# A two-layer graph network with a mixture of experts: thirds, selection matrices, products and routing moved to other steps

## The chip, the cores and the metric

The kernel runs on one core of a Trainium2 chip. The core has five engines that work side by side, each through its own instructions in order: TensorE (PE in the profile; its weight loads are PEld), VectorE (DVE), ScalarE (ACT), GpSimd (POOL) and SyncE (SP), which issues transfers. They wait for each other by semaphores. Times are microseconds (us) on the device. The number to be predicted is the median time of the changed kernel; the kernel before has a median of 3390.55 us over 3 runs (3386.48 to 3399.7).

## The reference, cut to what matters

There are 6250 nodes with 512 features, 100,000 edges sorted by their destination, and 8 experts.

```python
def _sage_layer(h, src, dst, W_self, W_neigh, b, n_nodes):
    agg = segment_sum(h[src], dst, n_nodes)
    deg = segment_sum(ones_like(dst), dst, n_nodes)
    h_neigh = agg / maximum(deg, 1.0)[:, None]
    return relu(h @ W_self + h_neigh @ W_neigh + b)

x = x + sage_layer2(sage_layer1(layernorm(x)))
xf = layernorm(x)                       # again, then a mixture of experts
logits = xf @ Wg
topv, topi = top_k(logits, 2)
gate_w = softmax(topv)
h = relu(xf @ W1[e] + b1[e])            # per expert e
y = h @ W2[e] + b2[e]
y = (y - mean) / sqrt(var + EPS) * gamma[e] + beta[e]
x = x + sum over the two chosen experts of gate_w * y
```

## The kernel before, in words

**Stages.** A first pass (up to about 117 us) normalizes the nodes and makes tables of the edges. Then `sums` runs twice: in stage 1 over the rows of the normalized nodes (layer 1, from about 120 to 1115 us), in stage 2 over the projected rows of layer 1 (layer 2, from about 1138 to 2340 us). A tail computes the remaining expert tiles and combines.

**What `sums` does.** The 782 tiles of 128 edges are taken in 197 steps of four tiles (`while` loop from L300). In step i GpSimd issues the gathers of step i + 2 (`gather`, L220): each fetches 128 rows of 512 numbers. The buffers of gathered rows form a ring, so a gather waits until `add` of three steps before has read its buffer. `build` (L230) makes, on VectorE, the zero-one matrices ("hot") of step i + 2. `add` (L248) multiplies them with the gathered rows on TensorE: each tile gives up to 32 destination rows, and the four tiles of a step lie under each other in one bank of PSUM, pa. Three steps make a round, 66 rounds in all. At the end of a round `close` copies pa into a bf16 strip on ScalarE (L258). `rest` makes the second and third strip out of what rounding left (L272 on VectorE, L273 on ScalarE, L274 on VectorE), so that three bf16 thirds hold the f32 sum. When a round is the last that can touch a block b of 128 nodes, `prepare` makes the block's selection matrices on VectorE (L280, one for each of its two to four rounds), and `take_out` multiplies the strips by them on TensorE (L290), two steps after the round has closed. In stage 1 `take_out` writes to a tile ps and also takes the degrees (pn); in stage 2 it writes to a tile named ph.

**What sets the order.** The order on TensorE, VectorE, ScalarE and GpSimd is the order of the code (`manual_schedule`). Work that follows later is put into a table with a step and a place: `at(i, place, what)`. In every step the loop issues the gathers, lets `each(i)` register new work, builds, adds, runs the "mid" list of that step, closes a round, and runs the "post" list. Within one list the work stands in the order in which it was registered, so what was registered longest ago comes first.

**Layer 1** (`layer1`) registers the products with the layer's weights after a take-out (u0 to u5, L557 and the transposes at L194).

**Layer 2** (`route`) follows each take-out of stage 2. VectorE finishes the block's rows (L1003, L1004), their mean and variance (L182, L184), ScalarE the root (L186), and VectorE the normalized rows xn (L187, L1011). Then `turn` transposes xn on TensorE (L194, copied by ScalarE at L196), `logits` multiplies by Wg (L958, copied at L960), `experts` transposes the logits and chooses two experts on VectorE and ScalarE (L964, L966, L654 to L669), `rank` counts the nodes of each expert (L976, L977 on TensorE; L979 to L987 on VectorE), and `send` scatters the rows to the experts' lists by GpSimd (L991). The tiles that logits, experts and rank write are all named small, with one bank.

**Expert tiles in stage 2** (`each`, `Up`, `Down`). As soon as enough lists are known (at step 76), an expert tile of 128 rows begins at every second step. `Up.fetch` reads the rows xg by SP (L812), `turn_x` transposes them (L194, L196), `times` is the up product (L824, eight TensorE passes, into a tile ph; copied by ScalarE to h at L827), `turn_h` transposes h (L832) and adds the bias with a relu on VectorE (L835). Every second tile ("soon") goes on at once: `Down` builds its on VectorE (L847), `times` is the down product (L858, eight passes, and L852 for the row b2, into py), `spread` takes mean and variance on VectorE (L864, L866) with a root on ScalarE (L868), `scale` normalizes (L871, L873, then L876 on ScalarE), `affine` makes the rows of gamma and beta on TensorE (L852, into two tiles ph) and `finish` multiplies and adds them on VectorE (L882, L883) and stores y by SP. The other tiles keep hT in memory for the tail. PSUM tiles named ph come in two buffers, those named pt in two.

**Share of layer 2.** Until step 48, `share_of` (L923) multiplies the stored layer 1 rows in three steps of four.

The registrations that the change touches are these, before:

```python
at(i + 1, "mid", lambda pa=pa[0]: rest(st, k, pa))
at(i + 1, "mid", lambda b=b: prepare(b))
at(i + 2, "mid", lambda b=b: take_out(i + 2, b))
todo = [(2, "mid", turn), (3, "mid", logits), (4, "mid", experts), (5, "post", rank), ...
todo = [(0, "post", u.fetch), (3, "mid", u.turn_x), (4, "mid", u.times), (5, "mid", u.turn_h)]
todo += [(7, "mid", begin), (8, "mid", spread), (9, "mid", scale), (10, "post", affine and finish)]
```

Of the kernel before, what the change touches and what calls it, by code (L numbers as in the profile page):

```python
# [29 lines left out]
F32 = mybir.dt.float32  # L30
# [9 lines left out]
P = 128  # L40
# [27 lines left out]
def gnn_moe(ctx, tc, x, src, dst, Ws1, Wn1, gb1, Ws2, Wn2, gb2, Wg, W1, b1, W2, b2, gamma, beta, out):  # L68
    nc = tc.nc
    N, D = x.shape  # L70
# [4 lines left out]
    HC = H // P  # L75
# [124 lines left out]
    def sums(z, pool, pap, room, pn, finish, ring, nring, each=None):  # L200

        nslot = (NG - 1) * TS + min(TS, NT_E - (NG - 1) * NQ * TS)
        ahead = nring // NQ - 1
        tiles = [[t for t in range(i // TS * NQ * TS + i % TS, min(NT_E, (i // TS + 1) * NQ * TS), TS)]
                 for i in range(nslot)]
        gathered, hots, few, strips, counts, sels, due = {}, {}, {}, {}, {}, {}, {}  # L210
        pa = [None]

        def at(i, place, what):
            due.setdefault((i, place), []).append(what)

        def gather(i):
            if i < nslot:
                for t in tiles[i]:
                    gathered[t] = ring()
                    nc.gpsimd.indirect_dma_start(  # L220
                        out=gathered[t], out_offset=None, in_=z[:, :],
                        in_offset=bass.IndirectOffsetOnAxis(ap=srcT[:, t : t + 1], axis=0))

        def build(i):
            if i >= nslot:
                return
            g, j = divmod(i, TS)
            m = len(tiles[i])
            hots[i] = pool.tile([P, NQ, SW], F32, name="hot", bufs=3 if pn is None else 4)
            nc.vector.tensor_tensor(  # L230
                hots[i][:, :m],
                rel.rearrange("p (c j) -> p j c", j=TS)[:, j, g * NQ : g * NQ + m]
                .rearrange("p (t o) -> p t o", o=1).to_broadcast([P, m, SW]),
                iota_row[:, :SW].rearrange("p (o m) -> p o m", o=1).to_broadcast([P, m, SW]), OP.is_equal)
            if pn is not None and j:

                end = j == TS - 1 or i == nslot - 1
                few[g] = pool.tile([P, NQ, SW], BF16 if end else F32, name=f"few{int(end)}", bufs=1)
                before = hots[i - 1] if j == 1 else few[g, 1]
                nc.vector.tensor_add(few[g][:, :m], before[:, :m], hots[i][:, :m])  # L240
                few[g, j] = few[g]

        def add(i):
            g, j = divmod(i, TS)
            if pa[0] is None:
                pa[0] = pap.tile([P, D], F32, name="pa", bufs=2)
            for q, t in enumerate(tiles[i]):
                nc.tensor.matmul(pa[0][q * SW : (q + 1) * SW], hots[i][:, q], gathered.pop(t), start=(j == 0),  # L248
                                 stop=(j == TS - 1 or t == NT_E - 1), tile_position=(0, q * SW))

        def close(i):

            g = i // TS
            k = len(tiles[i]) * SW

            st = [pool.tile([P, D], BF16, name=f"st_{h}", bufs=most) for h in range(3)]
            strips[g] = st, k
            nc.scalar.copy(st[0][:k], pa[0][:k])  # L258
            at(i + 1, "mid", lambda pa=pa[0]: rest(st, k, pa))
            pa[0] = None  # L260
            if pn is not None:
                nc.tensor.matmul(pn[:k, 0], few[g].rearrange("p q m -> p (q m)")[:, :k], halves,
                                 start=True, stop=True)
                counts[g] = pool.tile([P, NDEG], BF16, name="counts", bufs=most + 1)
                nc.vector.tensor_copy(counts[g][:k], pn[:k, 0])
            for b in range(NB):
                if reach[b][1] == g:
                    at(i + 1, "mid", lambda b=b: prepare(b))
                    at(i + 2, "mid", lambda b=b: take_out(i + 2, b))

        def rest(st, k, pa):
            nc.vector.tensor_sub(pa[:k], pa[:k], st[0][:k])  # L272
            nc.scalar.copy(st[1][:k], pa[:k])  # L273
            nc.vector.tensor_sub(st[2][:k], pa[:k], st[1][:k])  # L274

        def prepare(b):
            for g in range(reach[b][0], reach[b][1] + 1):
                k = strips[g][1]
                sels[b, g] = pool.tile([P, P], BF16, name="sel", bufs=most)
                nc.vector.tensor_scalar(sels[b, g][:k], iota_row[:k], float(b * P), node[:k, g : g + 1],  # L280
                                        op0=OP.add, op1=OP.is_equal)

        def take_out(i, b):
            a, z = reach[b]
            ps = room()
            for g in range(a, z + 1):
                st, k = strips[g]
                sel = sels.pop((b, g))
                for h in range(3):
                    nc.tensor.matmul(ps, sel[:k], st[h][:k], start=(g == a and h == 0), stop=(g == z and h == 2))  # L290
                if pn is not None:
                    nc.tensor.matmul(pn[:, 1], sel[:k], counts[g][:k], start=(g == a), stop=(g == z))
            for behind, place, what in finish(b, ps) if pn is None else finish(b, ps, pn[:, 1]):
                at(i + behind, place, what)

        for i in range(ahead):
            gather(i)
        build(0)
        build(1)
        i = 0  # L300
        while i < nslot or any(k[0] >= i for k in due):
            gather(i + ahead)
            if each is not None:
                for behind, place, what in each(i):
                    at(i + behind, place, what)
            build(i + 2)
            if i < nslot:
                add(i)
            for what in due.pop((i, "mid"), ()):
                what()  # L310
            if i < nslot:
                if i % TS == TS - 1 or i == nslot - 1:
                    close(i)
            for what in due.pop((i, "post"), ()):
                what()
            i += 1
# [111 lines left out]
    with tc.tile_pool(name="l0", bufs=3, side="right") as pool, \  # L428
# [4 lines left out]
        for lo, hi in ((NS, NB), (0, NS)):  # L433
            full = hi if rows[hi - 1] == P else hi - 1
            at = lo
# [405 lines left out]
    class Down:  # L841
# [10 lines left out]
            nc.tensor.matmul(ps, self.its, thirds[name], start=to is None, stop=True)  # L852
            return ps

        def times(self):
            self.py = self.psp.tile([P, D], F32, name="py", bufs=1 + (self.rows["beta"] == "pb"))
            for c in range(HC):
                nc.tensor.matmul(self.py, self.hT[:, c], w2[:, bass.ds(self.e * KD + c * D, D)],  # L858
                                 start=(c == 0), stop=False)
            self.row("b2", self.py)  # L860

        def spread(self):
            st = self.pool.tile([P, 6], F32, name="st")
# [23 lines left out]
    rest = [i for i in range(NT) if i not in soon]  # L887
# [7 lines left out]
    def fetch_hidden(k):  # L895
        nc.sync.dma_start(part(NW + k % NE), hd[rest[k]])

    with tc.tile_pool(name="s2", bufs=2, side="right") as pool, \
# [32 lines left out]
        def ring():  # L931
            nring[0] += 1
            return part(NW + (nring[0] - 1) % 12)
# [10 lines left out]
        def route(b, pa):  # L944
# [61 lines left out]
            for e in range(NE):  # L1006
                if b == (1 + 3 * e if e < NE // 2 else NB // 4 - 3 + e):
# [2 lines left out]
            t["xn"] = part(NW + (13, 14, 16)[b % 3])  # L1010
            nc.vector.tensor_scalar(t["xn"][:n], acc[:n], mv[:n, 0:1], rs[:n], op0=OP.subtract, op1=OP.mult)  # L1011
            fetch_own(b + 1)
            todo = [(2, "mid", turn), (3, "mid", logits), (4, "mid", experts), (5, "post", rank),
                    (7, "mid", lambda: send(0)), (7, "post", lambda: send(1))]
            if b + 1 in TAKE:
                todo.append((7, "post", take))
# [2 lines left out]
        def each(i):  # L1019


            at_slot[0] = i
            if i == last_slot + 1:
                for k in range(EARLY):
                    fetch_hidden(k)
            q = i - 1 - i // 4
            if i % 4 and q < NS:
                return [(0, "post", lambda: share_of(q))]
            j = up_next[0]
            if i % 2 or j >= upto_n[-1]:  # L1030
                return []
            c = max(c for c in range(len(n0)) if n0[c] <= j)
            if ready.get(c, 1 << 30) > i:
                return []
            up_next[0] += 1
            u = Up(j, pool, psp, keep=j not in soon)
            todo = [(0, "post", u.fetch), (3, "mid", u.turn_x), (4, "mid", u.times), (5, "mid", u.turn_h)]
            if j in soon:
                d = {}

                def begin():
                    d[0] = Down(j, u.hT, u.e, pool, psp, pool.tile([P, D], F32, name="y", bufs=1))
                    d[0].rows = {"gamma": "ph", "beta": "ph"}
                    d[0].times()

                todo += [(7, "mid", begin), (8, "mid", lambda: d[0].spread()), (9, "mid", lambda: d[0].scale()),
                         (10, "post", lambda: (d[0].affine(), d[0].finish()))]
            return todo

        for q in range(3):  # L1050
# [319 lines left out]
```

## Time and profile before

| What | Value |
|---|---|
| median of 3 runs | 3390.55 us (3386.48 to 3399.7) |
| the profiled execution's own time | 2960.86 us |
| its span, first to last instruction | 2958.9 us |
| mean granted TensorE clock | 0.971 |
| TensorE busy | 2647.7 us, 89% of the span |
| GpSimd busy | 1840.5 us, 62% |
| VectorE busy | 1344.7 us, 45% |
| ScalarE busy | 682.4 us, 23% |
| bytes moved | 699.16 MB, mean 236 GB/s |

The profile is of one execution, whose own time is 430 us below the median of the runs shown. In its rows, a line number such as L248 is a line of the kernel, out<-in names the tiles written and read, x is a number of instructions. "Idle before" is the time that an engine stood still just before instructions of that row, with what it waited for behind the arrow; "issue" means that no cause shows. In a list of waits, the numbers are microseconds in total, how often, and the longest. A timeline row has its start, its length and the idle time before it in brackets. A TensorE row's end is modelled, so a row may reach a little into the next. The granted clock is a share of full speed.

### The profile page before, as it was taken

To read this page: it belongs to the slowest core of one execution; us is meant where nothing else is said; L and a number is where in the kernel's file an instruction comes from. 1 tells how busy PE (TensorE), PEld (TensorE's weight loads), DVE (VectorE), ACT (ScalarE), POOL (GpSimd) and SP (SyncE) were. 2 spreads that over 40 slices of the span, in tenths; PEclk is the share of its full clock that TensorE was granted. 3 is DMA by queue.
4 is the path that set the end of the run, shared out by engine and by line. 5 is a ranking of instruction groups with operands and counts; after the bars stand their busy time and mean duration, and the time that the engine had idled before them with its cause. 6 is when DMAs were issued, how large, how long until landed. Compare 5 with 4: busy or idle time off the path is not lost. (4 is left out here: it accounts for less than half of the span.)

```text
span 2958.9 us, 34414 instructions
## 1 busy us (share of the span) xinstructions
PE 2647.7 (89%) x10010; PEld 1035.4 (35%) x10010; DVE 1344.7 (45%) x4274; ACT 682.4 (23%) x1259; POOL 1840.5 (62%) x2116
## 2 busy tenths in 40 slices
PE   6889999999999998999878999899898889999994
PEld 3323333333333333333212333333333333344441
DVE  6523233323323331454335556555655536544774
ACT  2311111111112120121112333333333312222221
POOL 5377777777777763777777777677677118200553
PEclk8999999999999998999989999999999999999997
DMA  6778888888887765999888888888788424212996
GB/s 226 248 238 250 250 250 248 271 245 254 244 252 235 238 205 182 328 327 316 274 280 272 279 271 274 254 271 273 248 273 269 148 84 146 92 57 75 297 299 206
DMA packets 269820, 699.16 MB, mean 236 GB/s; under 512 B 43036, under 2 KB 43150, under 8 KB 269596
## 3 DMA queue, kind: packets, MB, share of 16 engines
q0 software_dynamic: 144000, 464.43, 50.9%
q1 hardware_dynamic: 121964, 225.61, 22.1%
q10 hardware_dynamic: 3664, 6.85, 0.7%
q8 instruction: 85, 1.39, 0.2%
q14 instruction: 107, 0.88, 0.1%
HBM read 557.23 MB, written 140.28 MB: 236 GB/s over the span
## 5 line engine op out<-in xcount | busy, mean ns | idle before, releaser
L220 POOL DMA_INDIRECT big<-z,srcT x782 | 749.6, 959 | 334.5 <-issue 150.1
L220 POOL DMA_INDIRECT rows_t<-xn_d,srcT x782 | 741.1, 948 | 285.2 <-issue 126.7
L248 PE MATMUL pa<-big,hot 128*32 128x512 f32 x1564 | 335.2, 622 | 58.0 <-DMA big<-z,srcT 53.3
L557 PE MATMUL pm<-wn,tT 128*128 128x512 f32 x752 | 347.7, 605 | 0.7 <-ACT tT L196 0.7
L248 PE MATMUL pa<-rows_t,hot 128*32 128x512 f32 x1564 | 275.3, 608 | 24.6 <-DMA rows_t<-xn_d,srcT 23.8
L824 PE MATMUL ph<-big,xg 128*128 x544 | 258.5, 619 | 42.3 <-ACT xg L196 42.0
L1093 POOL DMA_INDIRECT big<-ys,yrow x98 | 107.8, 1100 | 291.2 <-DMA ys<-y 193.1
L858 PE MATMUL py<-w,hT 128*128 x568 | 263.6, 607 | 5.8 <-DVE hT L1146 5.6
L557 PEld LDWEIGHTS pm<-wn,tT 128*128 128x128 f32 x752 | 135.2, 189 | 214.2 <-issue 168.9
L274 DVE TENSOR_TENSOR st<-pa,st 128x512 bf16<-128x512 f32 x132 | 91.2, 691 | 214.3 <-ACT st L273 209.6
L273 ACT CAST st<-pa 128x512 bf16<-128x512 f32 x132 | 77.2, 585 | 416.6 <-DVE pa L272 416.6
L824 PEld LDWEIGHTS ph<-big,xg 128*128 128x128 f32 x544 | 100.5, 195 | 197.3 <-issue 130.4
L858 PEld LDWEIGHTS py<-w,hT 128*128 128x128 f32 x568 | 102.7, 191 | 144.2 <-issue 111.8
L290 PE MATMUL ps<-st,sel 128*128 128x512 bf16 (+1 forms) x459 | 110.2, 379 | 45.8 <-DVE sel L280 45.8
L991 POOL DMA_INDIRECT xs<-big,slot x98 | 98.6, 1006 | 77.2 <-DVE slot L987 47.9
L557 PE MATMUL pm<-ws,big 128*128 128x512 f32 x320 | 146.4, 602 | 0.0
L923 PE MATMUL ph<-w 128*128 128x512 f32 x288 | 135.8, 615 | 5.0 <-DMA w<-in_L_gnn_W_self 5.0
L1134 PE MATMUL ph<-big,xg 128*128 x296 | 136.9, 605 | 0.0
L248 PEld LDWEIGHTS pa<-big,hot 128*32 128x32 f32 x1564 | 51.2, 109 | 234.1 <-DMA big<-z,srcT 165.5
L858 PE MATMUL py<-w,big 128*128 x272 | 127.3, 611 | 4.8 <-DVE y L883 3.8
L290 PEld LDWEIGHTS <-sel 128*128 128x128 bf16 (+1 forms) x918 | 75.8, 98 | 157.6 <-DVE sel L280 63.3
L230 DVE TENSOR_TENSOR hot<-rel,iota_row 128x128 f32<-128x128 bf16 (+1 forms) x394 | 109.7, 283 | 31.2 <-PE pa L248 24.3
(265 smaller groups left out, 3335.0 us busy)
## 6 DMA issues: line engine op xcount, KB each, us to landing
xg<-xs SPq DMA_DIRECT2D x105, 256.0 KB, 4.1
ys<-y SPq DMA_DIRECT2D x105, 256.0 KB, 3.0
rows_t<-xn_d,srcT POOLq DMA_INDIRECT x782
big<-z,srcT POOLq DMA_INDIRECT x782
z<-big SPq DMA_DIRECT2D x48, 256.0 KB, 3.8
xa<-in_x SPq DMA_DIRECT2D x48, 256.0 KB, 5.7
big<-s SPq DMA_DIRECT2D x48, 256.0 KB, 5.4
accs<-xa SPq DMA_DIRECT2D x48, 256.0 KB, 3.9
```

The costliest lines, as they stand in the source:

```text
L220: nc.gpsimd.indirect_dma_start(out=gathered[t], out_offset=None, in_=z[:, :], in_offset=bass.IndirectOffsetOnAxis(ap=srcT[:, t : t + 1], a ...
L230: nc.vector.tensor_tensor(hots[i][:, :m], rel.rearrange("p (c j) -> p j c", j=TS)[:, j, g * NQ : g * NQ + m] .rearrange("p (t o) -> p t o" ...
L248: nc.tensor.matmul(pa[0][q * SW : (q + 1) * SW], hots[i][:, q], gathered.pop(t), start=(j == 0), stop=(j == TS - 1 or t == NT_E - 1), tile ...
L274: nc.vector.tensor_sub(st[2][:k], pa[:k], st[1][:k])
L290: nc.tensor.matmul(ps, sel[:k], st[h][:k], start=(g == a and h == 0), stop=(g == z and h == 2))
L557: nc.tensor.matmul(ph, tT[:, c], w[:, c], start=(start and c == 0), stop=(stop and c == C - 1))
L824: nc.tensor.matmul(ph, self.xT[:, c], w1[:, bass.ds(self.e * KD + c * D, D)], start=(c == 0), stop=(c == C - 1))
L858: nc.tensor.matmul(self.py, self.hT[:, c], w2[:, bass.ds(self.e * KD + c * D, D)], start=(c == 0), stop=False)
L923: nc.tensor.matmul(ps, hT[:, c], ws2[:, c], start=(c == 0), stop=(c == C - 1))
L991: inst = nc.gpsimd.indirect_dma_start(out=xs[:, :], out_offset=bass.IndirectOffsetOnAxis(ap=slot[:n, b, k : k + 1], axis=0), in_=t["xn"][: ...
L1093: nc.gpsimd.indirect_dma_start(out=yk[:n], out_offset=None, in_=ys[: ready[0] * P, :], in_offset=bass.IndirectOffsetOnAxis(ap=yrow[:n, b, ...
L1134: nc.tensor.matmul(ph, u.xT[:, c], w1[:, bass.ds(u.e * KD + c * D, D)], start=(c == 0), stop=(c == C - 1))
```

## The change

The loop gets a third list, "pre", which is run after `each(i)` and ahead of `build(i + 2)` and `add(i)`. These things move:

- `rest` (the second and third strips) goes from the "mid" list of the next step to its "pre" list.
- `prepare` (the selection matrices) goes from the "mid" list of the next step to the "post" list of the step in which the round closes.
- `turn`, `logits` and `experts` of a block go from steps 2, 3 and 4, "mid", to steps 1, 2 and 3, "post". `rank` and `send` stay.
- `Up.fetch` goes from step 0 to step 1, the up product from 4 to 5, `turn_h` from 5 to 6; `turn_x` stays at 3.
- `Down` begins at 7, "post", with the first four passes of its product; the other four and the row b2 follow at 8, "mid". `spread` goes to 8, "post", `scale` to 9, "post", `affine` and `finish` from 10, "post", to 11, "mid".

```diff
-            at(i + 1, "mid", lambda pa=pa[0]: rest(st, k, pa))
+            at(i + 1, "pre", lambda pa=pa[0]: rest(st, k, pa))
...
-                    at(i + 1, "mid", lambda b=b: prepare(b))
+                    at(i, "post", lambda b=b: prepare(b))
...
+            for what in due.pop((i, "pre"), ()):
+                what()
             build(i + 2)
...
-        def times(self):
-            self.py = self.psp.tile([P, D], F32, name="py", bufs=1 + (self.rows["beta"] == "pb"))
-            for c in range(HC):
+        def times(self, half=None):
+
+            if half != 1:
+                self.py = self.psp.tile([P, D], F32, name="py", bufs=1 + (self.rows["beta"] == "pb"))
+            for c in range(HC) if half is None else range(half * HC // 2, (half + 1) * HC // 2):
                 nc.tensor.matmul(self.py, self.hT[:, c], w2[:, bass.ds(self.e * KD + c * D, D)],
                                  start=(c == 0), stop=False)
-            self.row("b2", self.py)
+            if half != 0:
+                self.row("b2", self.py)
...
-            todo = [(2, "mid", turn), (3, "mid", logits), (4, "mid", experts), (5, "post", rank),
+            todo = [(1, "post", turn), (2, "post", logits), (3, "post", experts), (5, "post", rank),
...
-            todo = [(0, "post", u.fetch), (3, "mid", u.turn_x), (4, "mid", u.times), (5, "mid", u.turn_h)]
+            todo = [(1, "post", u.fetch), (3, "mid", u.turn_x), (5, "mid", u.times), (6, "mid", u.turn_h)]
...
-                    d[0].times()
-
-                todo += [(7, "mid", begin), (8, "mid", lambda: d[0].spread()), (9, "mid", lambda: d[0].scale()),
-                         (10, "post", lambda: (d[0].affine(), d[0].finish()))]
+                    d[0].times(0)
+
+                todo += [(7, "post", begin), (8, "mid", lambda: d[0].times(1)), (8, "post", lambda: d[0].spread()),
+                         (9, "post", lambda: d[0].scale()),
+                         (11, "mid", lambda: (d[0].affine(), d[0].finish()))]
```

## The prediction

> **What bounds the kernel now.** I read the totals, then busy time by stage, the gather groups, TensorE's waits by stage, and last the timeline of one repeat of the second sums. First the totals, then stages 1 (sums of layer 1), 2a and 2b (sums of layer 2 without and with expert tiles), with columns of length, busy time (instructions) of PE, PEld, DVE, ACT, POOL, granted clock, DMA share and GB/s:
>
> ```profile
> PE 2647.7 (89%) x10010; PEld 1035.4 (35%) x10010; DVE 1344.7 (45%) x4274; ACT 682.4 (23%) x1259; POOL 1840.5 (62%) x2116
> ```
> ```profile
> 120.00:1115.00 995.00, 928.48 (x3741) 341.37 (x3742) 295.48 (x910) 176.35 (x322) 739.07 (x780) 0.99 0.79 243
> ...
> 1310.00:1620.00 310.00, 258.67 (x917) 79.17 (x915) 134.52 (x505) 61.02 (x112) 236.28 (x269) 0.92 0.87 288
> 1620.00:2340.00 720.00, 647.32 (x2867) 268.87 (x2867) 410.58 (x1511) 240.60 (x423) 489.09 (x564) 0.98 0.81 261
> ```
>
> 89% busy looks like a TensorE bound, but GpSimd's gathers, in the timeline, start every 1.25 us (0.95 of work, 0.30 between). The 782 of stage 1 make 978 us of 995: stage 1 runs at the gathers' pace. In 2a TensorE waits for gathers too. In 2b GpSimd waits for TensorE:
>
> ```profile
> L220 POOL DMA_INDIRECT big<-z,srcT x443 | 424.6, 959 | 181.2 <-issue 91.8 <-PE pa L248 64.5 <-PE ph L824 6.1
> ```
>
> 64.5 us in 63 waits, of which 63 x 0.30 is the usual gap: some 45 us are left. That is all that 2b can gain before it too runs at the gathers' pace. TensorE's waits, stage 1 first (total, times, longest), then 2b:
>
> ```profile
> PE ps L290 <- DVE sel L280: 45.8, 35, 1.6
> ```
> ```profile
> PE ph L824 <- ACT xg L196: 32.8, 20, 4.1
> PE py L852 <- DVE its L847: 11.2, 4, 6.3
> PE pt L194 <- ACT xg L196: 11.0, 16, 0.7
> PE small L958 <- DVE fill L980: 6.5, 8, 0.8
> PE ph L852 <- ACT h L827: 5.5, 16, 0.4
> PE ph L852 <- DVE big L1003: 5.2, 10, 0.5
> ```
>
> These are the waits that the change moves. The last two tell more: gamma's and beta's products (L852) wait until the bank of an earlier up product or take-out has been read. All things named ph share **two banks in turn**, each free only when its second-last user was read.
>
> **A repeat of 2b.** Take-outs fall on steps 1, 4, 7 of every 12 (up to step 175; on 10, 4, 7 after it), an expert tile starts every second step, its down product every fourth. Twelve steps take 72.3 us (the same L824 wait starts at 1887.28, 1959.61, 2031.93); GpSimd needs 48 x 1.25 + 6 sends x 1.30 = 67.9. TensorE's waits in one repeat: 1.42 twice, 0.69 twice, 0.81, 0.53, so 5.6; its work 66.7.
>
> **The change, part by part.**
>
> *Thirds and selection matrices earlier.* Same instructions. In stage 1 the 45.8 us go: selections come a step sooner, and 0.69 + 0.58 + 0.69 of thirds start a step's work sooner. But the stage keeps its gathers' pace, TensorE then waits for rows: worth 0, with 1 to 2 us in the drain after the last gather. Queued behind the thirds on VectorE are the next hot matrices, used two steps on (hidden, unless VectorE lags two steps), and in stage 2 all of that step.
>
> *Up tile (fetch, up product, hT a step later).* The waits for xg go: 2 x 1.42 + 2 x 0.69 = 4.2 per repeat. The fetch on SP, 0.34 to issue and at most 5.9 to land, still follows the up product that frees its buffer, and now has one step and an add plus an up product (some 10 us) instead of two steps. Other SP transfers of that step (xa, sa, accs, ys) go ahead of it or beside it; 0, and up to 2 us a tile if that cover went. POOL's queue keeps its order: the sends stay. A gather waits only for the add three steps before, so later adds slow it, nothing else.
>
> *Halves.* Eight passes and the b2 row stay the same; 3.7 us of PE is split over two steps, its wait on its (11.2, all in two bookkeeping steps) gets more cover. Worth 0 to -2 in all; spread moves with them.
>
> *Gamma and beta: here is the cost.* Affine and finish move from (10, post) to (11, mid). Registered 11 steps ahead, they now come first in that list, and straight behind them the up product (registered 5 ahead), in the order gamma, beta, up. With two ph banks **the up product waits until VectorE has multiplied y by gamma (L882)**. Before, the next user of ph was a step away. VectorE works in order, so the wait is whatever VectorE has before L882. The row it has after each take-out (ending 1934.07):
>
> ```profile
> 1934.11 0.75 DVE L1003 SCALAR_TENSOR_TENSOR big<-ph,rcnt,big 128x512 f32<-128x512 f32 x1 [1.90 <-PE ph L290]
> ...
> 1936.89 0.16 DVE L187 RECIPROCAL rs<-rs 128x1 f32<-128x1 f32 x1 [0.36 <-ACT rs L186]
> 1937.09 0.55 DVE L1011 TENSOR_SCALAR big<-xa,mv,rs 128x512 f32<-128x512 f32 x1
> 1937.55 0.28 DVE L230 TENSOR_TENSOR hot<-rel,iota_row 128x128 f32<-128x128 bf16 x1
> ```
> ```profile
> 1957.53 0.15 DVE L966 COPY lg<-small 128x8 f32<-128x8 f32 x1
> ...
> 1959.49 0.16 DVE L669 TENSOR_TENSOR wts<-d,wts 128x1 f32<-128x1 f32 x1
> ```
>
> Take-out's end to xn is 3.55 (first four rows), the choice of experts with its exp 2.1 (last two). Counted from the take-out's end:
> - Step 1 (VectorE free): L882 0.69 plus 0.2 of signals after gamma, less beta 0.37: **0.5**.
> - Step 5, after take-out 4: 3.55 + experts 2.1 + hot 0.28 + L882 0.69 = 6.6; TensorE has the small transpose 0.2, add 1.07, gamma and beta 0.75: **4.5**.
> - Step 9, after take-out 7: 3.55 + scale 0.36 + experts 2.8 (with a table load on ACT, 1.28) + hot 0.28 + hT 1.13 = 8.1, then the thirds now ahead of L882: 0.69 + 0.58 + 0.69 = 10.1, hot 0.28, L882 0.69: 11.1. TensorE meanwhile: 0.2 + add 1.07 + hT's transposes 0.66, then the moved turning, which needs xn at 3.55 (**1.6** of wait) and takes 0.66, add 1.07, gamma and beta 0.75: 6.0. Wait **5.1**.
>
> *Turning and logits half a step nearer.* Besides that 1.6: rank of the block before and logits now stand together in the same list (steps 6 and 9; small has one bank), so logits wait for L979 and L980 instead of having an add between. At step 6 VectorE first has thirds, hT and bn_stats: **2.0**; at step 9 **0.5**. The 0.81 of before goes into these. In 2a the same pair, some 14 times, is mostly idle time that TensorE has there: +5.
>
> New per repeat: 0.5 + 4.5 + 5.1 + 1.6 + 2.0 + 0.5 = 14.2, old 5.6. The bound from below for gamma's wait is 0.5 each (VectorE always free): 1.5 per repeat instead of 10.1. I take the queue's rows, since VectorE does nothing out of order in them.
>
> *Rule and row: the clock.* After a long wait the next product is slow:
>
> ```profile
> 2222.69 5.24 PE L824 MATMUL ph<-big,xg 128*128 x8 [4.08 <-ACT xg L196]
> ```
>
> Eight passes take 3.70 otherwise: 1.5 more. The granted clock was 0.72 here, and 0.72, 0.50 and 0.62 around the other three waits above 3.8 us of 2b: four of four. The Trainium skill (TensorE: Matmul & The Clock Gate, "What's actually happening") says that an idle window of about 3.4 us halves the clock, until one such window was busy, and that the windows run freely; so a wait of 4.5 or 5.1 trips it with (4.5 - 3.4)/3.4 and (5.1 - 3.4)/3.4, together 0.8 times, at up to 1.7: an estimate of 1.4 per repeat. By the row 2 x 1.5 = 3.0. I take the row.
>
> **Sum.** Per repeat 14.2 - 5.6 + 3.0 = +11.6. Affine begins at step 89 and sums end at 197: 9 repeats, +104 (by the rule +90). Steps 76 to 89: 0. The last VectorE bookkeeping (step 164) now falls before a step like 9: +5. Drain with tiles alone: xg waits of 3.3, 2.5 and five of 0.69 go, six gamma waits of 0.5 and a last step come: -5. Stage 2a +5, stage 1 -2. Together +107 on the profiled execution's 2960.9 us (span 2958.9): 3068.
>
> The median shown, 3390.6, is 430 above that execution, by something that the trace does not show. If it were slower matmuls (430 of 2648, 16%), stage 1's 928 would become 1077, over the gathers' 978: its 45.8 would then be worth up to 46, 2a would cost some 10 more, and each wait would hide 1 us more work: about -9. 107 - 46 + 10 - 9 = +62. Between +62 and +107 I take **+80: 3470 us** (2.4% slower), own range 3430 to 3520.
>
> **Rivals.**
> 1. *Gain, at the gathers' pace* (faster, 0.12). VectorE reaches L882 early, so that gamma costs 0.5, and the old waits go. Deciding point: new waits under 5.6 per repeat. Then 2b gains at most 4.4 x 9 = 40, with stage 1's end 42: 3349; with slow matmuls also 46: about 3303. For it: VectorE is busy only 57% of 2b. Against: the take-out's chain stands right ahead of gamma at two of three places.
> 2. *Waits change places* (same, 0.08). Half of the queue is absent, the new 14.2 become 6 to 7 with no clock dip: -5 to +15, 3386 to 3406. For it: TensorE's wait at one place gives VectorE time at the next.
> 3. *Two banks don't bind*, because ph of gamma and of the up product are not one ring: then rival 1. Against: the two L852 waits above.
> 4. *Up product too late for hT and half* (inside slower): hT at 6, half at 7, no wait shown; +0.
>
> Chances: faster 0.12, same 0.08, slower 0.80, with 0.5% (17 us) as about what a measurement of this kernel can tell from no change. The range 3395 to 3520 leaves out rival 1 and half of rival 2 (0.16) and a few in 100 above.
>
> **What would show it.** Right: waits of PE ph L824 for DVE y L882, 27 or more in 2b, two in three above 3 us, with clock dips; PE small L958 for DVE fill some 18 times; waits for ACT xg and DVE sel gone; stage 1 unchanged in length; a repeat of 12 steps near 84 us; GpSimd waiting for PE pa more. Wrong: no L882 wait, or repeats near 68. Waits for fetched xg would be a miss of another kind.

## The result and the profile after

The changed kernel takes **3481.39 us** (median of 5 runs, 3476.34 to 3495.52), the kernel before 3386.48 beside it (3377.54 to 3399.7): ratio **1.0284, 95% interval 1.0253 to 1.0315**. Predicted were 3470 us and 2.4% slower; measured were 2.8%.

In one comparison all runs of this program were either of condition A, in which the kernel before takes about 2963 us at a granted clock of 0.97 (the trace that the prediction read), or of condition B, 3386 to 3409 us at 0.90 (the median that it started from, and the whole result), and every ratio below is formed within one of them.

The totals and the granted clock by slices (page of the changed kernel):

```profile
PE 2727.1 (78%) x10010; PEld 1092.3 (31%) x10010; DVE 1341.8 (38%) x4274; ACT 681.5 (20%) x1253; POOL 1835.6 (53%) x2116
...
PEclk9889888999899988888787888888888889999997
```

Where the time went, by the starts of the gathers, in two traces of condition B that were taken side by side (the last of each kernel). Gather 344 of stage 2 lies shortly ahead of the first product with gamma:

| Stretch, us | before | changed | difference |
|---|---|---|---|
| stage 1, first to last gather | 1167.6 | 1166.0 | -1.6 |
| stage 2, first gather to gather 344 | 560.0 | 577.9 | +17.9 |
| stage 2, gather 344 to the last | 848.3 | 900.0 | +51.7 |
| after the last gather | 664.4 | 677.3 | +12.9 |
| span | 3404.8 | 3486.0 | +81.2 |

(The other 0.3 us lie before stage 1 and between the stages.) Stage 1 kept its length, though its waits for selection matrices went. All of the loss is in stage 2 and behind it. The gather groups of stage 2 in the same two traces, before and then changed (busy time and mean ns, then idle time ahead and what ended it):

```profile
L220 POOL DMA_INDIRECT big<-z,srcT x782 | 748.3, 957 | 589.4 <-PE pa L248 245.3 <-issue 195.1 <-remote 64.0
```
```profile
L220 POOL DMA_INDIRECT big<-z,srcT x782 | 747.7, 956 | 659.7 <-PE pa L248 302.1 <-issue 189.2 <-remote 60.5
```

The gathers themselves cost the same; they wait 70 us longer, 57 of it for the adds on TensorE. What holds TensorE is seen in its waits over the whole changed kernel, here and in the next view in its first trace (total, times, longest):

```profile
PE ph L826 <- DVE y L887: 100.5, 22, 14.2
...
PE ph L826 <- issue: 29.2, 7, 5.0
...
PE ph L826 <- DVE hot L230: 26.4, 4, 6.6
PE small L963 <- DVE gk L990: 19.7, 6, 8.6
```

L826 is the up product (L824 before), L887 the multiplication by gamma (L882 before). The three L826 rows are one wait: the timeline has the same step of different repeats under the three names. Together they are 33 waits and 156 us (predicted: 27 or more for L887). No trace of before has a wait of L824 for L882. But in B the kernel before has waits of its up product too, first of all for ScalarE's copy of xg. By its three names they are 98.7 us in 31 waits:

```profile
PE ph L824 <- ACT xg L196: 56.0, 17, 8.2
...
PE ph L824 <- issue: 31.3, 6, 7.4
...
PE ph L824 <- ACT d L663: 11.4, 8, 1.4
```

One repeat of twelve steps, TensorE's long waits in brackets:

```profile
2301.58 6.59 PE L826 MATMUL ph<-big,xg 128*128 x8 [5.00 <-DVE y L887]
...
2330.50 5.78 PE L826 MATMUL ph<-big,xg 128*128 x8 [6.60 <-DVE y L887]
...
2362.67 6.77 PE L826 MATMUL ph<-big,xg 128*128 x8 [4.76 <-DVE y L887]
...
2378.23 0.92 PE L963 MATMUL small<-big,wg 128*8 128x128 f32 x7 [2.35 <-ACT rs L873]
...
2391.49 0.63 PE L194 MATMUL pt<-ident,big 128*128 128x128 f32 x4 [1.98 <-issue]
...
2399.31 5.52 PE L826 MATMUL ph<-big,xg 128*128 x8 [5.02 <-DVE y L887]
```

From step 9 (2301.58) to the next step 9 (2399.31) are 97.7 us. Each of the three up products behind gamma waits 4.8 to 6.6 us, and then its eight passes take 5.5 to 6.8 us instead of 3.70.

### The profile page after: what moved, and what is told of

Same layout as the page of the kernel before. It is cut to its first block, busy times and chain, and to the rows that moved or that the text cites. A ratio compares the mean times of both kernels' runs of the same rounds, so it can differ in the third digit from the quotient of the medians.

```text
span 3493.7 us, 34515 instructions
## 1 busy us (share of the span) xinstructions
PE 2727.1 (78%) x10010; PEld 1092.3 (31%) x10010; DVE 1341.8 (38%) x4274; ACT 681.5 (20%) x1253; POOL 1835.6 (53%) x2116
## 5 line engine op out<-in xcount | busy, mean ns | idle before, releaser
L826 PE MATMUL ph<-big,xg 128*128 x544 | 325.0, 752 | 156.0 <-DVE y L887 100.5
L559 PE MATMUL pm<-wn,tT 128*128 128x512 f32 x752 | 368.9, 636 | 41.8 <-ACT tT L196 28.9
L248 PE MATMUL pa<-big,hot 128*32 128x512 f32 x1564 | 287.0, 689 | 17.1 <-DMA big<-z,srcT 8.5
L248 PE MATMUL pa<-rows_t,hot 128*32 128x512 f32 x1564 | 237.1, 616 | 12.8 <-DMA rows_t<-xn_d,srcT 10.7
L826 PEld LDWEIGHTS ph<-big,xg 128*128 128x128 f32 x544 | 126.4, 245 | 359.5 <-issue 278.7
L290 PE MATMUL ps<-st,sel 128*128 128x512 bf16 (+1 forms) x459 | 137.3, 444 | 53.3 <-issue 53.3
L928 PE MATMUL ph<-w 128*128 128x512 f32 x288 | 153.8, 683 | 6.0 <-issue 6.0
L963 PE MATMUL small<-big,wg 128*8 128x128 f32 (+1 forms) x392 | 67.4, 330 | 109.2 <-issue 35.4
L837 DVE TENSOR_SCALAR hT<-pt,b1T 128x128 f32<-128x128 f32 x272 | 76.5, 343 | 159.8 <-PE pt L834 111.3
L1140 PE MATMUL ph<-big,xg 128*128 x296 | 136.9, 605 | 0.0
L272 DVE TENSOR_TENSOR pa<-pa,st 128x512 f32<-128x512 f32 x132 | 92.5, 701 | 113.0 <-ACT st L258 77.4
```

The source lines that it names most:

```text
L559: nc.tensor.matmul(ph, tT[:, c], w[:, c], start=(start and c == 0), stop=(stop and c == C - 1))
L826: nc.tensor.matmul(ph, self.xT[:, c], w1[:, bass.ds(self.e * KD + c * D, D)], start=(c == 0), stop=(c == C - 1))
L928: nc.tensor.matmul(ps, hT[:, c], ws2[:, c], start=(c == 0), stop=(c == C - 1))
L1140: nc.tensor.matmul(ph, u.xT[:, c], w1[:, bass.ds(u.e * KD + c * D, D)], start=(c == 0), stop=(c == C - 1))
```

## The experiments

None of these kernels leaves anything out of the work. The first four ran in condition A.

**The kernel before, once more.**

> The kernel before, unchanged, for a second trace. The trace of the changed kernel spans 3493.7 us at a mean clock of 0.881, and its stage 1 takes some 1190 us, where the trace of before had 2958.9, 0.971 and 995. Theory (two kinds of execution): the kernel before usually runs like that too, its trace will span about 3385 us at a clock near 0.88 with stage 1 near 1180, and the 430 us that its median stood above its trace are that. Rival (the change did it): stage 1 stays near 995 us and the clock near 0.97.

Measured: 2969.6 us, with 2962.9 for the other runs of before beside it: condition A was met again.

**Gamma and beta behind the up product.** The changed kernel with one word changed: gamma and beta stay in step 11, but come behind its up product:

```diff
-(11, "mid", lambda: (d[0].affine(), d[0].finish()))]
+(11, "post", lambda: (d[0].affine(), d[0].finish()))]
```

> The changed kernel with affine and finish at (11, post) in place of (11, mid): gamma and beta then come behind the up product, not ahead of it. Theory (the up product waits for gamma's bank): its waits for L887 (100.5 us in the changed kernel's trace, and the slow products after them) go, and the time comes down from 1.028 to between 0.99 and 1.01 of before. Rival (turning and logits half a step nearer, with the bank small, cost the time): 1.02 to 1.03, as changed.

Measured: ratio to before 1.004, 1.0026 to 1.0054 (2975.9 us). TensorE's longest waits of stage 2b (1620 to 2340 us) in this kernel:

```profile
PE small L963 <- DVE gk L990: 20.2, 8, 3.8
PE pt L194 <- DVE rs L876: 18.0, 9, 2.0
PE pt L194 <- DMA xg<-xs: 8.9, 8, 1.4
```

No up product waits for L887 any more. What is left are the two waits of the nearer routing that the prediction had named: logits behind rank, and turning before xn is there (9 times 2.0). The third row is new as well: the later fetch of an expert tile's rows is no longer quite covered, about once a repeat. Most repeats take about 75 us, against 72.3 before.

**Turning, logits and experts back; gamma still ahead.**

```diff
-todo = [(1, "post", turn), (2, "post", logits), (3, "post", experts), (5, "post", rank),
+todo = [(2, "mid", turn), (3, "mid", logits), (4, "mid", experts), (5, "post", rank),
```

> The changed kernel with turning, logits and experts back at (2, mid), (3, mid), (4, mid). Theory (gamma's bank): by the sum of the prediction 4.1 of 14.2 us of new waits per repeat go, of which the turning's 1.6 was itself cover for gamma's: 1.015 to 1.028 of before. Rival (the nearer routing): 0.99 to 1.005.

Measured: 1.0413, 1.0395 to 1.043 (3085.8 us). The waits of 2b, then the up product at steps 5, 9 and 1 of one repeat:

```profile
PE ph L826 <- DVE y L887: 129.7, 24, 14.2
```
```profile
2007.26 5.36 PE L826 MATMUL ph<-big,xg 128*128 x8 [2.89 <-DVE y L887]
...
2037.46 5.62 PE L826 MATMUL ph<-big,xg 128*128 x8 [6.75 <-DVE y L887]
2063.75 6.11 PE L826 MATMUL ph<-big,xg 128*128 x8 [4.89 <-DVE y L887]
```

The loss is larger than both expectations. The routing waits are gone, and gamma's alone make repeats of 85.4 to 88.0 us (longer where VectorE has its bookkeeping). Without the turning's wait ahead of it, step 9 waits 6.75 in one piece, and step 1, for which the prediction's sum had 0.5, waits 4.89.

**The sums' part alone, on the kernel before.**

```diff
-at(i + 1, "mid", lambda pa=pa[0]: rest(st, k, pa))
+at(i + 1, "pre", lambda pa=pa[0]: rest(st, k, pa))
...
-at(i + 1, "mid", lambda b=b: prepare(b))
+at(i, "post", lambda b=b: prepare(b))
```

> The kernel before with only the thirds at (1, pre) and the selection matrices at (0, post). Theory of the prediction for executions like the first trace: no gain in stage 1, 0.998 to 1.002. For executions in which stage 1 is slower than the gathers' pace: the 45.8 us of TensorE's waits for sel are worth something, 0.985 to 0.997.

Measured: 1.0172, 1.0155 to 1.0189 (3015.4 us): a clear loss where I had put nothing. Stage 1's gathers take 978.4 us, as before (978.3). TensorE's waits for sel are gone, and those for gathered rows have grown from 23.8 us to:

```profile
PE pa L248 <- DMA rows_t<-xn_d,srcT: 36.4, 47, 6.5
```

Most of the loss is in stage 2: from the first to the last gather 1159.2 us before, 1198.6 us here. Repeats take 74.9 to 77.9 us. Its place, VectorE and ScalarE at a step 8:

```profile
1956.12 0.70 DVE L272 TENSOR_TENSOR pa<-pa,st 128x512 f32<-128x512 f32 x1 [0.44 <-ACT st L258]
...
1957.47 0.69 DVE L274 TENSOR_TENSOR st<-pa,st 128x512 bf16<-128x512 f32 x1 [0.65 <-ACT st L273]
...
1958.47 0.21 DVE L875 TENSOR_SCALAR nm<-mv,rs 128x1 f32<-128x1 f32 x1
...
1958.72 0.78 ACT L878 ACTIVATE y<-py,nm,rs 128x512 f32<-128x512 f32 x1 [1.28 <-DVE nm L875]
1959.40 0.59 ACT L196 ACTIVATE xg<-pt 128x512 f32<-128x512 f32 x1
```
```profile
1960.04 1.11 PE L194 MATMUL pt<-ident,big 128*128 128x128 f32 x4 [3.25 <-ACT xg L196]
```

The thirds (L272, L274), ahead of everything on VectorE, hold up the small nm (L875); ScalarE, in order, stands at y for it; the copy of xg is behind y; and TensorE's next transposes wait 3.25 us for that copy's bank, where they waited 0.69 before. In 2b these waits were 11.0 us in 16 before, the longest 0.7; now they are:

```profile
PE pt L194 <- ACT xg L196: 31.4, 16, 3.3
```

One early piece of work goes through three queues, each in order, to the engine that counts.

**The same questions in condition B.** First the changed kernel again, as the base.

> The changed kernel itself beside the kernel before, on a chip where before takes 2963 us in its runs (if this chip is again such a one). Sum of the prediction on that time: +107, so 1.036. Its trace is then to be compared with the first trace of before. On a chip like that of the first comparison: 1.028.

Measured: 1.0285, 1.0225 to 1.0344. Then gamma behind and routing back together (both edits above):

> The changed kernel with affine at (11, post) and with turning, logits and experts back at (2, 3, 4, mid). e1 was 1.004 with 61 us of TensorE's waits of logits for rank and of turning for xn left. Theory (the nearer routing costs in its own right once gamma's wait is away): 0.990 to 1.000, held up by the gathers' pace, which allows 42 us. Rival (those waits are only time that the gathers need anyway): 1.002 to 1.006.

Measured: 0.9954, 0.9934 to 0.9974. Then the thirds back too, which leaves of the change only the up tile a step later, the halves with what follows them, gamma and beta one step later than before (but behind the up product), and the selection matrices earlier:

```diff
-at(i + 1, "pre", lambda pa=pa[0]: rest(st, k, pa))
+at(i + 1, "mid", lambda pa=pa[0]: rest(st, k, pa))
```

> As the kernel with affine behind and routing back, and the thirds back at (1, mid); the selection matrices stay at (0, post). e3 showed the sums' part alone at 1.017, all of it in stage 2. Theory (thirds ahead of everything on VectorE and ScalarE hold up the stage 2 work behind them): 0.984 to 0.993, 42 us being the most that the gathers' pace allows in stage 2. Rival (the selection matrices a step earlier are what cost in e3): no better than with the thirds at pre.

Measured: 0.984, 0.9793 to 0.9888. The thirds' new place costs 1.1 points in B, as 1.7 in A with the matrices' together.

**Gamma and beta in other banks.** This keeps every step of the changed kernel and takes only the shared bank away: the two rows are written to the two banks named pt, not ph.

```diff
-d[0].rows = {"gamma": "ph", "beta": "ph"}
+d[0].rows = {"gamma": "pt", "beta": "pt"}
...
+    to = self.psp.tile([P, C, P], F32, name="pt").rearrange("p c n -> p (c n)")
```

> The changed kernel with every step and place as in the change, but gamma's and beta's rows in the two pt banks in place of the two ph banks. Theory (the wait is for gamma's ph bank): TensorE's up products no longer wait for L887, gamma and beta wait for hT in a pt bank instead, up to 3 us in one step of 12: 1.005 to 1.02. Rival (VectorE comes too late with everything, whatever bank): 1.03 or more.

Measured: 1.0062, 1.0043 to 1.0081. The wait of L826 for L887 is not in the trace (L826 waits 1.0 us in all); part of it has become waits of gamma's own product for those banks, which the transposes use too (two of TensorE's waits in 1700 to 2440 us; the product is at L855 here):

```profile
PE pt L855 <- issue: 34.2, 11, 10.8
...
PE pt L855 <- DVE hT L837: 10.2, 3, 3.4
```

So of the 2.8 points of loss the ph bank alone holds 2.2, with the new waits for pt already set off against it. From gather 344 of stage 2 to the last, where gamma acts, this kernel takes 833.9 us, less than the 848.3 of the kernel before; what it still loses lies ahead of gather 344 (583.1 us against 560.0).

**The best version again, with the changed kernel and the kernel before beside it.**

> The changed kernel again. So far the kernel before took 2963 us in one set of runs (clock 0.97) and 3386 and 3409 in two others (clock 0.90), each steady throughout its set; the changed one was seen in the slow sets alone, 1.028 both times. In a set like the first: the prediction's sum gives 1.036; what e2 (1.041 there, with less of the change) and the trace's third wait for gamma (6.6 us at step 1 where 0.5 was counted) point to is 1.045 to 1.055. In a slow set: 1.028.

Measured: 1.0243, 1.0214 to 1.0272.

> The kernel that was 0.984 in a slow set, again. In a set like the first one TensorE's waits in stage 2 are worth at most the 42 us down to the gathers' pace: 0.986 to 0.995. In a slow set: 0.984.

Measured: 0.98, 0.9773 to 0.9827 (3334.7 us, where before takes 3402.3). This kernel beats both in B; it was not run in A. Stretch 1700 to 2440 us of the changed kernel, then of this one (length; busy time and instructions of PE, PEld, DVE, ACT, POOL; granted clock, DMA share, GB/s):

```profile
1700.00:2440.00 740.00, 510.56 (x2094) 203.41 (x2090) 304.02 (x1142) 173.05 (x303) 422.06 (x483) 0.81 0.67 209
```
```profile
1700.00:2440.00 740.00, 575.63 (x2353) 220.54 (x2351) 333.01 (x1255) 194.86 (x341) 465.62 (x532) 0.87 0.73 231
```

In the same time TensorE does 2353 instructions instead of 2094, at a clock of 0.87 instead of 0.81.

> The kernel before, unchanged, for a trace in the condition of this set. In a slow set its stage 1 will take about 1180 us as that of the changed kernel does (theory: the 430 us are the condition's), or about 995 (rival: the change made stage 1 slow).

Measured: span 3404.8 us at a clock of 0.900; it is the "before" of the table above. The waits for sel in B (78.3 us in 26, the longest 8.3) are longer than in A, and still nothing was won in stage 1 by taking them away.

**The sums' part undone in the changed kernel.** The two lines of "the sums' part alone", taken back, while gamma stays ahead. Condition A.

> The changed kernel with its sums part undone: thirds and take-out matrices are made one step later again, at their old place in the middle of the VectorE's list; gamma and beta still stand directly ahead of the up product, halves and routing stay as changed. If thirds ahead of everything are part of what makes the row of gamma late at steps 1 and 9, the wait of the up product at step 1 falls from 6.6 us to under 2 and the ratio to the kernel before is 1.010 to 1.020. If the sums have no part in it and the bank alone makes the loss, the wait at step 1 stays over 4 us and the ratio at 1.024 to 1.029. In stage 1 both expect the waits of the sums for sel to be back and the length of the stage to be what it was.

Measured: 1.0588, 1.057 to 1.0606 (3138.4 us): the worst ratio of all, and far from either number. Those had been set from condition B, so the ratio decides nothing between them; the waits do. One repeat, steps 5, 6, 8, 9 and 1:

```profile
2127.86 5.43 PE L826 MATMUL ph<-big,xg 128*128 x8 [4.94 <-DVE y L887]
...
2144.61 1.65 PE L963 MATMUL small<-big,wg 128*8 128x128 f32 x7 [4.88 <-DVE gk L990]
...
2158.05 0.63 PE L194 MATMUL pt<-ident,big 128*128 128x128 f32 x4 [1.98 <-DVE rs L876]
2158.61 1.92 PE L248 MATMUL pa<-big,hot 128*32 128x512 f32 x8
...
2163.24 6.50 PE L826 MATMUL ph<-big,xg 128*128 x8 [1.75 <-DVE y L887]
...
2189.84 5.14 PE L826 MATMUL ph<-big,xg 128*128 x8 [2.73 <-DVE y L887]
```

At step 9 the theory holds: 1.75 instead of the 5.02 of the changed kernel. At step 1 it falls: this wait is 4.13 to 4.24 us in five of seven repeats (2.73 in the one shown, 10.72 in one), not under 2. And at step 6 a new wait has come, logits for rank, 4.88 where the changed kernel has 2.35. VectorE shows why:

```profile
2140.77 0.69 DVE L272 TENSOR_TENSOR pa<-pa,st 128x512 f32<-128x512 f32 x1
...
2142.11 0.69 DVE L274 TENSOR_TENSOR st<-pa,st 128x512 bf16<-128x512 f32 x1 [0.65 <-ACT st L273]
2142.72 0.67 DVE L280 TENSOR_SCALAR sel<-iota_row,node 128x128 bf16<-128x128 f32 x3
...
2144.38 0.23 DVE L990 TENSOR_TENSOR gk<-eqs,rk 128x8 f32<-128x8 bf16 x2
```

Thirds and matrices, 2.7 us from 2140.77 on, now stand ahead of the rank whose reading frees the bank that logits need. The early thirds had taken them out of that place. A repeat is 92.2 us (2127.86 to 2220.03). At both places that were tried for the thirds, some wait of TensorE is behind them, as gamma or rank stands directly ahead of its bank's next user.

## Why the prediction was right, and where its terms were off

**Stage 1 at nothing: right, but only in A for the reason given.** In A the gathers keep their pace (978.4 us against 978.3) and the waits for rows grow. In B the difference is -1.6 us as well, but there the stage is far from that pace (1166.0 us), and the waits for rows stay at 10 us. TensorE's waits from 120 to 1283 us are 245 us before and 239 us changed; those of the transposes L194 grew from 90 to 127 us while those for sel went. The prediction had put up to 46 us of gain on slower executions; why none came is open.

**Gamma's bank sets the up product: right, and it is the cause.** "VectorE has multiplied y by gamma" is the wait in the trace, and with other banks alone the loss falls from 2.8 to 0.6 points. Rivals 1 and 3 are out by this. Rival 2 is out in its size, since the wait does not fade because TensorE stands still elsewhere; but in B something of it is true, as the old waits of the up product were 98.7 us there. Rival 4 left nothing to see in the changed kernel. Waits for fetched xg, which the prediction called a miss of another kind, are two in its first trace ahead of the tail (1.49 and 2.52 us); with gamma out of the way they were eight, 8.9 us in all (first experiment with an edit).

**The single waits:**

| Place | predicted | the repeat shown |
|---|---|---|
| step 5, gamma | 4.5 | 4.76 |
| step 9, gamma | 5.1 | 5.02 |
| step 8, turning | 1.6 | 1.98 |
| step 6, logits | 2.0 | 2.35 |
| step 9, logits | 0.5 | 0.46 |
| step 1, gamma | 0.5 | **6.60** |

Five of six are within 0.4 us, though of condition B, which the sum was not worked out for. (By the prediction's own terms step 5 is 4.6, not 4.5.) The one that failed is "Step 1 (VectorE free)". Before the change no long wait of TensorE lay there, and I read that as an idle VectorE. In fact a round's thirds come at that step too. VectorE in the changed kernel, up to gamma's multiplication:

```profile
2325.44 0.70 DVE L272 TENSOR_TENSOR pa<-pa,st 128x512 f32<-128x512 f32 x1 [3.38 <-issue]
...
2326.79 0.69 DVE L274 TENSOR_TENSOR st<-pa,st 128x512 bf16<-128x512 f32 x1 [0.65 <-issue]
...
2327.62 1.11 DVE L837 TENSOR_SCALAR hT<-pt,b1T 128x128 f32<-128x128 f32 x4
...
2329.68 0.68 DVE L887 TENSOR_TENSOR y<-y,ph 128x512 f32<-128x512 f32 x1
```

From the first third to L887's end are 4.9 us of queue, and with the thirds in their old place the wait is of the same kind (4.13, last experiment). Ahead of it VectorE stood 3.38 us for a strip that was late on ScalarE. In A, without that, step 1 waits 4.89 (routing back).

**The clock dips: right in kind, sized at 3.0 us where 8.0 came.** Predicted were 3.0 us per repeat by the row, 1.4 by the rule. In the repeat shown the three products take 6.59 + 5.78 + 6.77 - 3 x 3.70 = 8.0 us more than their work: three waits instead of two, and 2.1 to 3.1 us each where the row had 1.5. The wait for turning, only 1.98 us, brings the clock down as well. Here it is in the last experiment, in stretches of 3.41 us (length; busy time and instructions of PE, PEld, DVE, ACT, POOL; granted clock, DMA share, GB/s):

```profile
2155.27:2158.68 3.41, 1.43 (x16) 0.92 (x16) 2.84 (x11) 0.72 (x2) 1.64 (x3) 1.00 0.91 317
...
2158.68:2162.09 3.41, 2.81 (x10) 0.24 (x10) 2.33 (x14) 2.81 (x5) 2.67 (x3) 0.50 0.77 239
2162.09:2165.51 3.42, 2.27 (x3) 1.17 (x4) 2.39 (x6) 0.00 (x0) 2.63 (x3) 0.50 0.85 286
2165.51:2168.92 3.41, 3.41 (x5) 1.35 (x4) 0.00 (x0) 0.00 (x0) 1.15 (x2) 0.50 0.82 269
2168.92:2172.33 3.41, 3.01 (x12) 1.35 (x10) 0.90 (x3) 1.56 (x3) 0.00 (x0) 1.00 0.25 88
```

In the first stretch TensorE stands for 1.98 us, and the clock falls at its end. The next two hold gamma's wait of 1.75 us, the third is busy throughout, and behind it the clock is full again: 10.2 us at half, in which the add takes 1.92 us instead of 1.06 and the up product 6.50. The Trainium skill (TensorE: Matmul & The Clock Gate, "What's actually happening") speaks of an idle window of about 3.4 us ahead of half clock, and of one busy window to come back. The second agrees with these rows. The first does not: 1.98 us idle in one stretch were enough, so the measurement decides, and an estimate from a whole idle window was too low.

**The repeat.** With these two terms corrected the sum comes close: 72.3 - 5.6 of old waits + 21.2 (the table) + 8.0 = 95.9, where the repeat shown has 97.7. It has a wait of 1.46 for its besides; the adds slowed behind the shorter waits are not counted, so it closes to a few us only. My 84 was for condition A. There the two other kernels with gamma ahead of the up product have 85.4 to 88.0 (routing back) and 92.2 (sums' part undone).

**Why +80 was near the +95 all the same: in part luck.** With the waits and dips of the repeat shown, nine repeats against 72.3 us would have lost 9 x (21.2 - 5.6 + 8.0) = 212 us, twice the +104 of the sum. From gather 344 on the measured loss is 51.7 us. The reason is that the kernel before, in B, does not have repeats of 72.3 us: they are 92.0 to 95.6, the changed kernel's 96.0 to 98.7 (both without the bookkeeping steps). One of its up products waits about 7.3 us in nearly all of them, and its eight passes then take 6.7; the change took this away, where the prediction had booked 4.2 for all waits for xg. On the other side are 17.9 us ahead of gather 344, where gamma has no part and the sum had +5, and 12.9 us after the last gather, where it had -5. The 17.9 rest on one trace of before in B: three of the changed kernel lie 11 to 23 us above it, the three versions with the routing back -8 to +9, so the nearer routing is suspected and not shown. So the sign and its cause are the prediction's, and the nearness of the sum is not.

The prediction allowed for the unknown 430 us with "slower matmuls", by up to -45 of which it took -27. That was not what B is: the eight passes take 3.70 us there too when the clock is full, and TensorE's busy time in stage 1 is within 2% of the 928.48 us of A. Stretch 120 to 1310 us of the kernel before in B:

```profile
120.00:1310.00 1190.00, 945.75 (x3746) 352.31 (x3746) 293.37 (x914) 178.00 (x323) 741.99 (x780) 0.91 0.68 203
```

The work is the same; the waits are longer (up to 11.5 us in this stretch where A has 6.5), and the data come at 203 GB/s instead of 243. What makes them longer stays open. In condition A, the changed kernel would by the two kernels nearest to it (1.0413 and 1.0588) have lost more than in B; it was not run there, and this stays an inference.

**Thirds earlier: a cost in stage 2 that the sum did not have.** "Queued behind the thirds on VectorE are the next hot matrices, used two steps on (hidden, unless VectorE lags two steps), and in stage 2 all of that step" named the queue, but the sum put nothing on it, and the text missed nm and with it ScalarE's order: 39 of the 52 us that the sums' part alone costs in A lie between the gathers of stage 2. In B the thirds' place costs 1.1 points of ratio.

**Up tile a step later, halves: right in sign.** They are what remains in the version at 0.98 of before, together with the earlier matrices and the later gamma; these were not taken apart.

## What to carry to other kernels

When a product is moved so that it stands directly ahead of another user of the same ring of banks, cost it as a wait of TensorE for the whole queue of the engine that reads the bank: list that queue's instructions one by one at every step of the repeat, also at those where the old trace shows no wait. Work that is brought forward to "ahead of everything" on a half-busy engine is not free; follow what stands behind it through each in-order queue (here VectorE's thirds, nm, ScalarE's y, xg, a bank, TensorE). Other banks, or one place further behind, were worth more here than an earlier start. And before adding new waits to an old trace, see whether that trace has the time of the runs that are to be predicted: here its repeats were 20 us shorter.

## What the runs showed of the hardware that was not expected

**Short waits and the clock.** In every trace here the granted clock is 1.00 or 0.50, and its changes lie whole multiples of 3.41 us apart (in the changed kernel 2327.92, 2334.75, 2362.05, 2368.88). The first trace of the changed kernel, cut into such stretches over its whole length, gives this: the 110 stretches at full clock that were followed by half clock had TensorE busy (matmuls or weight loads) for 0 to 55% of them, the 662 that were followed by full clock for 43% or more. Of the stretches at half clock, the 109 that were followed by full clock were busy for 78% or more, the 132 others for 90% or less. So in this trace about half a stretch of standing still brings half clock for the next, and a stretch that is nearly all busy gives it back. It fits the single cases: 1.42 us idle (before, 1887.28 and 1959.61) left the clock at 1.00; 1.98 us (last experiment, 2158.05) and 2.35 us (changed kernel, 2378.23) brought it to 0.50 within a microsecond of the work that followed.
